# The second attention's scores in float32r: exact halves of q and k, copied through device memory

## The chip, the cores and the metric

One NeuronCore of a Trainium2 chip runs the whole program. The metric is the time of one execution on the device in microseconds. Engines are named as in the profile: PE (matrix products), PEld (its weight loads), DVE and ACT (element-wise work and reductions, both can read PSUM), POOL (GpSimd, SBUF only), SP (issues DMAs).

## The reference

An input `x` of 16 sequences of 256 tokens with 128 features goes through four residual layers: a first attention (2 heads of 64 features, rotated positions), a gated FFN, a second attention, and the same FFN once more.

```python
x = x + attn_a(layernorm(x))
x = x + ffn(layernorm(x))
x = x + attn_b(layernorm(x))
x = x + ffn(layernorm(x))
```

The second attention has 16 heads of 8 features. Its mask lets key k go with query q where k <= q, and a masked score is set to -10000. Cut to what matters:

```python
qkv = encodings @ attn_w.T + attn_b             # 16 heads of q, k, v with 8 features each
mask = arange(n)[:, None] <= arange(n)[None, :]
scores = einsum('bhki,bhqi->bhkq', k, q) / sqrt(8)
scores = where(mask, scores, -10000.0)
probs = softmax(scores, axis=2)                 # axis 2 is k: over the keys of each query
combined = einsum('bhkq,bhkl->bhql', probs, v)
out = combined.reshape(b, n, 128) @ out_w.T + out_b
```

The FFN has a hidden width of 512, three layers of ternary weights before the last product, and runs twice with the same weights.

## The kernel before, in words

Tokens are worked on in eight iterations of 512 (`TOK`), which are two sequences each (`s` = 0, 1). The residual `x` stays in SBUF (`XR`).

**A plan sets the order.** Nothing is issued as it is written. The body records operations with a guessed duration each, for example `p("PE", 1.2, ...)`. `Plan.laid` then places them in time on five engines, one after the other: an operation can start when its inputs have ended (plus `HOP`, or the `lag` given with it), its engine is free and a slot of its pool is free. Among those that could start on an engine about equally early it takes the one with the lowest number of `order_of`, which reads the table `ORDER`. `WEIGH` says how far a change of mode (an activation table on ACT, an array shape on PE) counts in this choice, `SWITCH` and `LOAD` what it costs. `p.either` leaves the choice between engines to the plan. `emit` then issues everything in that order, so each engine has a fixed queue. Since `emit` issues nearly all instructions, they all carry one line in the profile (L287), and operations are told apart by their tiles.

**Names in the profile.** Buffer numbers are left out, so `w` is a large work slot (`w4`, `w6`, `w8`) or a one-bank PSUM tile. `s` is the only score tile: four banks of PSUM, one slot, used by both attentions. `h` are the FFN's hidden parts, `h_sb` its weights, `hl` the FFN's last hidden layer, `m` the row maxima, `q` (with `s`) the tile `q2`.

**The FFN** splits its inputs into a rounded float32r part and the float32r rest (`parts`), and multiplies both with the float32r weights, in products of 512 columns. A branch at the end of the setup chooses between this and a version for weights that float32r can't hold; the execution profiled took the first.

**The second attention** (`attention_b_inputs`, `attention_b_max`, `attention_b`) has three steps in an iteration.

1. Inputs. A layernorm, a transpose, and the products of q, k and v in f32, each evicted from a PSUM bank. Four heads share 32 rows (8 features each). To single out one head, k is evicted four times, each time scaled by a mask `kmask` that leaves one head's features, with extra rows set to one; q is evicted twice (`qscale`). These tiles sit in `g_16` (q) and `g_32` (k).
2. Maxima, per sequence. For each of four head positions `a`: scores of four groups `g` at once, in four bands of 32 rows of the array (f32, 128 queries by 128 keys and 128 by 256), then a bf16 product with `hide` that adds a very negative number where the mask forbids. DVE reduces the tile to negated maxima (`m3`). When all four are done, small operations bring the maxima into `nm`, PE transposes it, and DVE adds it into the free rows of q, which gives `q2`.
3. Probabilities and sums, per sequence. Scores again, transposed (keys on the partitions) from k and `q2`, so that the maximum is subtracted by the product itself; ACT takes the exponential of the tile, POOL's `affine_select` zeroes what is masked on the diagonal blocks, and PE sums with `vp`.

A tile of scores holds three blocks of 128 by 128 per head (the fourth is all masked). The tiles of steps 2 and 3 take turns on the one score tile; the plan puts products of the FFNs (first `f`, then `g`) on PE in the waits.

**DMA queues.** SP issues the loads at the start and one store of `x` per iteration at the end. POOL issues the loads of the weights that are rounded to float32r on the way. After the loads nothing but the stores moves through DMA.

Of the kernel before, what the change touches and what calls it, by code (L numbers as in the profile page):

```python
# [94 lines left out]
class Plan:  # L95
# [4 lines left out]
    SWITCH = 0.15  # L100
    WEIGH = 0.78
# [64 lines left out]
    def laid(self):  # L166
# [28 lines left out]
        for _ in range(len(self.ops)):  # L195
            best = None
            for e, ops in ready.items():
# [23 lines left out]
                if not cands:  # L221
                    continue

                first = min(a + self.WEIGH * c for a, c, _ in cands)
                at, cost, op = min(
                    (x for x in cands if x[0] + self.WEIGH * x[1] <= first + 0.144),
# [63 lines left out]
class _Recorder:  # L290
# [47 lines left out]
    (INPUT, "a"): (47, 0.9),  # L338
    (MAIN, "a"): (52, 1.0),
    (NORM, "f"): (298, 0),  # L340
    (FILL, "f"): (118, 3.3),
    (INPUT, "b"): (76, 0.9),
    (MAXIMA, "b"): (-22, 0),
    (MAIN, "b"): (14, 17.0),
    (NORM, "g"): (81, 0),
    (FILL, "g"): (180, 9.1),
}
LATER_AT = -89
# [23 lines left out]
def hybrid_kernel(ctx: ExitStack, tc: tile.TileContext, x, rows, cols, wa, wb, w12, h1, h2, w3, out):  # L372
# [5 lines left out]

    p = Plan(nc)
# [13 lines left out]
    g_24, g_16, g_32 = group("w6", 4), group("w4", 3), group("w8", 3)  # L393
    q_qkv, q_pT, q_qkT, q_qb, q_pa, q_kb = Group(2), Group(3), Group(2), Group(2), Group(2), Group(2)
    g_rope, g_oT, g_small = group("rope", 6), group("oT", 2), group("small", 16)
    g_vb, g_q2, g_wv, g_o, g_oTb = (group(n, k) for n, k in (("vb", 2), ("q2", 2), ("wv", 2), ("o", 2), ("oTb", 1)))
# [166 lines left out]

    pi = fixed([P, 4], "pi", I32)
    p("POOL", 0.1).iota(pi[:], pattern=[[0, 4]], base=0, channel_multiplier=1)
    wanta = fixed([P, 4], "wanta", I32)
    p("POOL", 0.1).iota(wanta[:], pattern=[[1, 4]], base=0, channel_multiplier=0)
    wantr = fixed([P, 4], "wantr", I32)
    p("POOL", 0.1).iota(wantr[:], pattern=[[-3, 4]], base=31, channel_multiplier=0)
    ai = fixed([P, 4], "ai", I32)  # L570
    ri = fixed([P, 4], "ri", I32)
    kmask = fixed([P, 4], "kmask")
    mrow4 = fixed([P, 4], "mrow4")
    kbias = fixed([P, 4], "kbias")
    qscale = fixed([P, 2], "qscale")
    qbias = fixed([P, 2], "qbias")
    mrow = fixed([P, 2], "mrow")
    s8 = 1.0 / math.sqrt(DB)
    o = p("DVE", 1.25)
    o.tensor_scalar(ai[:], pi[:], 3, 3, ALU.arith_shift_right, ALU.bitwise_and)  # L580
    o.tensor_scalar(ri[:], pi[:], 31, None, ALU.bitwise_and)
    o.tensor_tensor(kmask[:], ai[:], wanta[:], ALU.is_equal)
    o.tensor_tensor(mrow4[:], ri[:], wantr[:], ALU.is_equal)
    o.scalar_tensor_tensor(kbias[:], kmask[:], cols_sb[:, C_BK : C_BK + 1], mrow4[:], ALU.mult, ALU.add)
    o.tensor_scalar(qscale[:, 0:1], kmask[:, 3:4], -s8, s8, ALU.mult, ALU.add)
    o.tensor_scalar(qscale[:, 1:2], kmask[:, 3:4], s8, None, ALU.mult)
    o.tensor_scalar(qbias[:], qscale[:], cols_sb[:, C_BQ : C_BQ + 1], None, ALU.mult)
    o.tensor_reduce(mrow[:, 0:1], mrow4[:, 0:3], AX.X, ALU.max)
    o.tensor_copy(mrow[:, 1:2], mrow4[:, 3:4])
# [137 lines left out]
    def attention_a(i, qkv, qkT):  # L727

        sc = p.tile(psum, [P, SEQS, HA, 2, T], F32, f"sa{i}", g_scores)
        for s in range(SEQS):  # L730
            o = p("PE", 0.87, "2r")
            for q in range(2):
                for h in range(HA):
                    hs = slice(h * DA, (h + 1) * DA)
                    c0 = s * T + q * P
                    o.matmul(
                        sc[:, s, h, q, :],
                        lhsT=qkT[hs, 0, c0 : c0 + P],
                        rhs=qkT[hs, 1, s * T : (s + 1) * T],
                        start=True,  # L740
                        stop=True,
                    )
# [59 lines left out]
    def attention_b_inputs(i):  # L802

        xT = layernorm_T(i, "b", ob[:])
        q = sb([P, 2, TOK], f"qb{i}", g_16, q_qb)
        pq = bank(f"pqb{i}", ahead)
        p("PE", 0.45, "1", claim=[q]).matmul(pq[:], lhsT=wb_sb[:, 0:128], rhs=xT[:], start=True, stop=True)
        for c in range(2):
            by, plus = qscale[:, c : c + 1], qbias[:, c : c + 1]
            p.either(  # L810
                ("DVE", 0.72, "tensor_scalar", (q[:, c, :], pq[:], by, plus, ALU.mult, ALU.add), {}),
                ("ACT", 0.67, "activation", (q[:, c, :], pq[:], AF.Identity), {"bias": plus, "scale": by}),
            )
        k = sb([P, 4, TOK], f"kb{i}", g_32, q_kb)
        pk = bank(f"pkb{i}", ahead)
        p("PE", 0.45, "1", claim=[k]).matmul(pk[:], lhsT=wb_sb[:, 128:256], rhs=xT[:], start=True, stop=True)
        for a in range(4):
            by, plus = kmask[:, a : a + 1], kbias[:, a : a + 1]
            p.either(
                ("ACT", 0.67, "activation", (k[:, a, :], pk[:], AF.Identity), {"bias": plus, "scale": by}),  # L820
                ("DVE", 0.72, "tensor_scalar", (k[:, a, :], pk[:], by, plus, ALU.mult, ALU.add), {}),
            )
# [8 lines left out]
        return q, k, v  # L831

    def attention_b_max(i, s, q, k, v):
# [10 lines left out]
        for a in range(4):  # L844
            c = a // 3

            sc = p.tile(psum, [P, 4, 512], F32, f"sb{n}_{a}", g_scores)
            o = p("PE", 1.2, ("4r", "1"))
            for qt, c0, w in ((0, 0, P), (1, P, T)):
                for g in range(4):  # L850
                    gs = slice(32 * g, 32 * g + 32)
                    o.matmul(
                        sc[:, g, c0 : c0 + w],
                        lhsT=q[gs, c, t0 + qt * P : t0 + (qt + 1) * P],
                        rhs=k[gs, a, t0 : t0 + w],
                        start=qt == 0,
                        stop=False,
                        skip_group_check=True,
                    )

            blocks = sc[:, :, 0:384].rearrange("p g (b k) -> p g b k", k=P)
            for g in range(4):
                o.matmul(
                    blocks[:, g, slice(0, 3, 2), :], lhsT=eye[:], rhs=hide[:], start=False, stop=True, skip_group_check=True
                )
            p("DVE", 1.68).tensor_reduce(
                m3[:, :, :, 3 - a].rearrange("p b g -> p g b"), blocks, AX.X, ALU.max, negate=True
            )
        nm = NMR[s]
        cols32 = nm[:].rearrange("p t (g r) -> p t g r", r=32)[:, :, :, 22:32:3]  # L870

        e0 = small([P, 2, 4, 4], f"e0{n}")
        m0 = small([P, 2, 4, 4], f"m0{n}")
        o = p("DVE", 0.4)


        o.tensor_scalar(cols32[:, 0], m3[:, 0], least[:, 0:1], None, ALU.min)
        o.scalar_tensor_tensor(cols32[:, 1], m3[:, 1], least[:, 1:2], m3[:, 2], ALU.min, ALU.min)
        o.tensor_scalar(m0, cols32, -NEG, None, ALU.min)
        p("ACT", 0.35, "exp").activation(e0, m0, AF.Exp, bias=neg[:])  # L880
        pm = bank(f"pm{n}")
        q2 = sb([P, 2, T], f"q2{n}", g_q2)
        o = p("PE", 0.15, "1", claim=[q2])
        for t in range(2):
            o.transpose(pm[:, t * P : (t + 1) * P], nm[:, t, :], ident[:])
        for c in range(2):
            p("DVE", 0.39).scalar_tensor_tensor(
                q2[:, c, :], pm[:, 0:T], mrow[:, c : c + 1], q[:, c, t0 : t0 + T], ALU.mult, ALU.add
            )
        return k, v, vp, e0, q2  # L890

    def attention_b(i, s, k, v, vp, e0, q2):
# [25 lines left out]
        for half in range(2):  # L918
            pTs = []
            for a2 in range(2):  # L920
                a = 3 - (2 * half + a2)
                c = a // 3


                st = p.tile(psum, [P, 4, 512], F32, f"st{n}_{a}", g_scores)
                blocks = st[:, :, 0:384].rearrange("p g (b q) -> p g b q", q=P)
                pT = sb([P, 3, 4, P], f"pT{n}_{a}", g_24, q_pT)
                o = p("PE", 0.66, "4r", claim=[pT])
                for kt, bs, w in ((0, slice(0, 3, 2), T), (1, slice(1, 2), P)):
                    for g in range(4):  # L930
                        gs = slice(32 * g, 32 * g + 32)
                        o.matmul(
                            blocks[:, g, bs, :],
                            lhsT=k[gs, a, t0 + kt * P : t0 + (kt + 1) * P],
                            rhs=q2[gs, c, T - w : T],
                            start=True,
                            stop=True,
                        )
                p("ACT", 1.38, "exp").activation(pT[:].rearrange("p b g q -> p g b q"), blocks, AF.Exp)
# [11 lines left out]
            for a2 in range(2):  # L951
                o = p("PE", 0.66, "4c", claim=[ps])
                for kt in range(2):
                    for g in range(4):
# [3 lines left out]
                            rhs=pTs[a2][:, slice(0, 3, 2) if kt == 0 else slice(1, 2), g, :],  # L958
# [42 lines left out]
    def product(po, w_sb, wv, os, high, low, nc_, claim, chain="ffn", part_of=None):  # L1001
# [15 lines left out]
        def general():  # L1017
            wl = []
            for c in range(nc_):
                wf = work.tile([P, P], F32, name="wf", tag="wf")  # L1020
                nc.sync.dma_start(out=wf[:], in_=wv[:, c, os])
                wl.append(work.tile([P, P], F32R, name=f"wl{c}", tag=f"wl{c}"))
                nc.gpsimd.tensor_tensor(wl[c][:], wf[:], w_sb[:, c, os].now(), ALU.subtract)
# [162 lines left out]
```

## Time and profile before

| | |
|---|---|
| time, median of 3 runs | 823.2 us (822.59 to 823.42) |
| the profiled execution | 823.35 us, of which its span is 821.6 us |
| granted clock of PE, mean | 0.983 |
| busy PE / DVE / ACT / POOL | 762.0 / 538.2 / 538.0 / 222.9 us |
| largest groups of PE | 281.2 us FFN products `w<-h,h_sb`; 71.4 us maxima scores `s<-w,w`; 71.2 us probability scores `s<-q,w`; 39.1 us mask `s<-hide,eye` |
| per score tile | 1755 ns reduction on DVE, 1452 ns exponential on ACT |
| table loads on ACT | 125, 160.4 us |
| DMA traffic | HBM read 8.53 MB, written 2.10 MB |

The span runs from the first to the last instruction. A group's row in the profile gives the line, the engine, the operation, output and inputs, the shape, the count, then busy time and mean duration of one, then the idle time before it and what ended that. Matmuls overlap with their successors, so the mean duration of one is longer than what it costs PE; the distance from start to start is the better measure. The rows of stages and of the order of time are explained where they are shown.

### The profile page before, as it was taken

What the parts mean: (1) busy time and instruction counts of PE and PEld (TensorE: products, weight loads), DVE (VectorE), ACT (ScalarE), POOL (GpSimd) and SP (SyncE); (2) the same over time, 40 slices, a digit from 0 to 9 for tenths busy, and PEclk for the clock granted to TensorE, in tenths of its full rate; (3) what the DMA queues carried; (4) which work ended last, traced back from release to release, by engine and by line L of the source; (5) the groups of instructions that cost most, each with busy time, mean ns of one, the idle gap of its engine ahead of it and who ended that gap; (6) DMA issues with size and microseconds to landing.
All of it is one profiled execution on the core that took longest, in us unless ns stands there. A gap on an engine that the chain in (4) does not pass through costs nothing.

```text
span 821.6 us, 15080 instructions
## 1 busy us (share of the span) xinstructions
PE 762.0 (93%) x6212; PEld 536.1 (65%) x6212; DVE 538.2 (66%) x1129; ACT 538.0 (65%) x744; POOL 222.9 (27%) x322
## 2 busy tenths in 40 slices
PE   4688999999999999999999998999999999999997
PEld 2355666667577676667675765776776577676775
DVE  7897866877778486637847775763773576262551
ACT  3455887745946746974687475549468546989743
POOL 7654444110411403320233033113113301323200
PEclk9689999999999999999999999999999999999999
DMA  9400000000000000000000000000000000000000
GB/s 286 130 2 1 1 2 0 2 1 1 2 1 1 1 2 1 1 2 1 1 2 2 1 1 2 2 14 2 14 1 14 2 1 14 1 14 1 14 15 18
DMA packets 12191, 11.69 MB, mean 14 GB/s; under 512 B 720, under 2 KB 9424, under 8 KB 12112
## 3 DMA queue, kind: packets, MB, share of 16 engines
q1 hardware_dynamic: 10624, 7.61, 3.0%
q0 software_dynamic: 1200, 2.62, 0.9%
q8 instruction: 51, 0.84, 0.4%
q10 hardware_dynamic: 288, 0.39, 0.3%
q14 instruction: 28, 0.23, 0.1%
HBM read 8.53 MB, written 2.10 MB: 13 GB/s over the span
## 4 chain that ended last, share of the span: by engine, by line
PE 60%; DVE 20%; ACT 14%; issue 2%; POOL 1%; DMA 1%; SPq 0%; POOLq 0%; DVEq 0%; ACTq 0%
PE w L287 45%; PE s L287 15%; ACT w L287 6%; ACT L287 5%; DVE w L287 4%; DVE h L287 2%; DVE small L287 2%; DVE xhattn L287 2%; ACT u L287 2%; DVE u L287 2%; DVE m L287 1%; DMA x<-in_x 1%; ACT h L287 1%; DVE o L287 1%; DVE xlffn L287 1%
## 5 line engine op out<-in xcount | busy, mean ns | idle before, releaser
L287 PE MATMUL w<-h,h_sb 128*128 128x512 f32 x1024 | 281.2, 412 | 3.7 <-DVE h L287 1.3
L287 PEld LDWEIGHTS w<-h,h_sb 128*128 128x128 f32 x1024 | 181.3, 189 | 56.0 <-issue 8.7
L287 ACT ACT_TABLE_LOAD x125 | 160.4, 1283 | 4.1 <-PEq L1177 1.3
L287 POOL TENSOR_SCALAR_AFFINE_SELECT w<-w 128x1024 f32<-128x1024 f32 x64 | 71.6, 1119 | 289.2 <-ACT w L287 282.9
L287 DVE TENSOR_REDUCE m<-s 128x12 f32<-128x1536 f32 x64 | 112.3, 1755 | 50.3 <-PE s L287 49.9
L287 ACT ACTIVATE u<-w,cols_sb 128x512 f32<-128x512 f32 x128 | 87.1, 687 | 76.5 <-PE w L287 75.9
L287 ACT ACTIVATE w<-s 128x1536 f32<-128x1536 f32 x64 | 92.9, 1452 | 32.1 <-PE s L287 30.7
L287 DVE TENSOR_TENSOR h<-u,h 128x512 fp32r<-128x512 f32 x105 | 74.9, 713 | 42.5 <-ACT h L287 39.8
L287 ACT ACTIVATE hl<-w,cols_sb 128x512 f32<-128x512 f32 x64 | 42.1, 687 | 53.7 <-PE w L287 53.4
L287 DVE SCALAR_TENSOR_TENSOR u<-w,cols_sb,u 128x512 f32<-128x512 f32 x64 | 47.7, 746 | 32.9 <-ACT u L287 26.6
L287 PE MATMUL s<-w,w 32*128 32x128 f32 (+1 forms) x1024 | 60.0, 348 | 3.9 <-DVE m L287 2.1
L287 PE MATMUL w<-w_sb,hl 128*128 128x128 f32 x512 | 63.1, 277 | 0.1
L287 PE MATMUL s<-q,w 32*128 32x256 f32 (+1 forms) x1024 | 59.8, 347 | 3.4 <-ACT w L287 2.7
L287 PEld LDWEIGHTS s<-q,w 32*128 32x128 f32 x1024 | 46.2, 184 | 25.5 <-ACT w L287 13.3
L287 PEld LDWEIGHTS w<-w_sb,hl 128*128 128x128 f32 x512 | 60.0, 192 | 2.8 <-ACT hl L287 1.9
L287 PE MATMUL w<-w,vp 128*32 128x256 f32 (+1 forms) x1024 | 55.3, 335 | 4.3 <-POOL w L287 2.8
L287 PE MATMUL w<-xTffn,w_sb 128*128 128x512 f32 x128 | 56.9, 445 | 2.2 <-DVE u L287 1.6
L287 DVE TENSOR_TENSOR x<-w,x 128x512 f32<-128x512 f32 (+1 forms) x40 | 23.2, 579 | 46.5 <-PE w L287 46.0
L287 PE MATMUL w<-xlffn,w_sb 128*128 128x512 f32 x128 | 52.5, 410 | 0.0
L287 PEld LDWEIGHTS s<-w,w 32*128 32x128 f32 x1024 | 34.3, 185 | 24.6 <-DVE m L287 8.9
L287 POOL TENSOR_TENSOR h<-u,h 128x512 fp32r<-128x512 f32 x23 | 29.6, 1290 | 65.3 <-ACT h L287 55.2
L287 PEld LDWEIGHTS w<-w,vp 128*32 128x32 f32 x1024 | 27.1, 110 | 29.5 <-issue 8.7
(153 smaller groups left out, 1068.2 us busy)
## 6 DMA issues: line engine op xcount, KB each, us to landing
w<-in_h SPq DMA_DIRECT2D x2, 1024.0 KB, 14.7
h_sb<-in_h POOLq DMA_DIRECT2D x2, 1024.0 KB, 11.6
out<-x SPq DMA_DIRECT2D x8, 256.0 KB, 2.3
x<-in_x SPq DMA_DIRECT2D x7, 256.0 KB, 8.0
w<-in_w SPq DMA_DIRECT2D x1, 512.0 KB, 8.8
w_sb<-in_w POOLq DMA_DIRECT2D x1, 512.0 KB, 7.2
rows_sb<-in_rows ACTq DMA_DIRECT2D x1, 384.0 KB, 7.1
x<-in_x SPq DMA_DIRECT2D x2, 128.0 KB, 3.2
```

The lines of the kernel that those rows point to most:

```text
L287: getattr(getattr(self.nc, self.ENGINES[op.engine]), name)(*a, **k)
```

## The change

The scores of the second attention are computed from float32r operands.

- **Halves.** q (already scaled by 1/sqrt(8) in its weights) and k are each evicted once into a float32r tile (the rounded part), and the rest is written beside it as a second float32r part. Two parts of q times two parts of k make four products.
- **Copies through device memory.** SP writes both parts, each twice, to a DRAM tile `far` (four DMAs per iteration, two for q and two for k). POOL reads `far` back (two DMAs per iteration) with rows ordered so that one head's 8 features stand in 32 rows four times, once for each pairing of parts. The result `t4` is `[P, 4, TOK]`: group `g` in the free dimension, head `a` in the band of 32 rows.
- **Scores.** All score products have 256 columns and use 32 rows; a tile of maxima has two sets of four, a tile of probabilities has two sets of four and two more that add the maxima: `pick` (ones in the rows of one group) times the transposed maxima `mT`, which are kept in two parts also. `q2`, `kmask`, `kbias`, `qscale`, `qbias` and `mrow` go.
- **Blocks.** The three used blocks of a tile stand next to each other in another order, so the mask is one run of 256 columns.
- **Pools.** `w8` has four slots in place of three and holds q and k; the small pool goes from 16 to 14 slots, the scratch of POOL's DMAs from 8192 to 4096. The branch for unrounded weights uses less memory.
- **The plan.** `ORDER`, `LATER_AT`, `WEIGH` (now by engine), `SWITCH` and the margin of equal starts have other values, and some guessed durations.

```diff
-    SWITCH = 0.15
-    WEIGH = 0.78
+    SWITCH = 0.17
+    WEIGH = {"ACT": 1.94, "PE": 0.13}
...
-                first = min(a + self.WEIGH * c for a, c, _ in cands)
+                weigh = self.WEIGH.get(e, 0.0)
+                first = min(a + weigh * c for a, c, _ in cands)
                 at, cost, op = min(
-                    (x for x in cands if x[0] + self.WEIGH * x[1] <= first + 0.144),
+                    (x for x in cands if x[0] + weigh * x[1] <= first + 0.038),
...
 ORDER = {
-    (INPUT, "a"): (47, 0.9),
-    (MAIN, "a"): (52, 1.0),
-    (NORM, "f"): (298, 0),
-    (FILL, "f"): (118, 3.3),
-    (INPUT, "b"): (76, 0.9),
-    (MAXIMA, "b"): (-22, 0),
-    (MAIN, "b"): (14, 17.0),
-    (NORM, "g"): (81, 0),
-    (FILL, "g"): (180, 9.1),
+    (INPUT, "a"): (-246, 24.6),
+    (MAIN, "a"): (-179, 7.8),
+    (NORM, "f"): (-106, 135.5),
+    (FILL, "f"): (-25, 25.2),
+    (INPUT, "b"): (47, 34.3),
+    (MAXIMA, "b"): (-415, 50.6),
+    (MAIN, "b"): (83, 10.6),
+    (NORM, "g"): (1714, 5.8),
+    (FILL, "g"): (1005, 103.1),
 }
-LATER_AT = -89
+LATER_AT = 124
...
-    g_24, g_16, g_32 = group("w6", 4), group("w4", 3), group("w8", 3)
+    g_24, g_16, g_32 = group("w6", 4), group("w4", 3), group("w8", 4)
...
     def attention_b_inputs(i):
         xT = layernorm_T(i, "b", ob[:])
...
-        for c in range(2):
-            by, plus = qscale[:, c : c + 1], qbias[:, c : c + 1]
+        tiles = []
+        for name, c0, bias in (("q", 0, C_BQ), ("k", P, C_BK)):
+            plus = cols_sb[:, bias : bias + 1]
+            pp = bank(f"p{name}b{i}", ahead)
+            hl = sb([P, 2, TOK], f"{name}hl{i}", g_16, q_hl, F32R)
+            p("PE", 0.45, "1", claim=[hl]).matmul(pp[:], lhsT=wb_sb[:, c0 : c0 + P], rhs=xT[:], start=True, stop=True)
             p.either(
...
+                ("ACT", 0.67, "activation", (hl[:, 0, :], pp[:], AF.Identity), {"bias": plus}),
+                ("DVE", 0.72, "tensor_scalar", (hl[:, 0, :], pp[:], plus, None, ALU.add), {}),
+            )
+            p("DVE", 0.77).scalar_tensor_tensor(hl[:, 1, :], pp[:], plus, hl[:, 0, :], ALU.add, ALU.subtract)
+            shape = [P, 2, 2, TOK]
+            far = p.fixed(dram.tile(shape, F32, name=f"far_{name}{i}"), shape)
+            for part in range(2):
+                p("SP", 0.55, lag=2.4).dma_start(
+                    out=far[:, part] if name == "q" else far[:, :, part],
+                    in_=hl[:, part, :].bitcast(F32).unsqueeze(1).to_broadcast([P, 2, TOK]),
+                )
+            t4 = sb([P, 4, TOK], f"{name}4{i}", g_32, None, F32R)
+            p("POOL", 0.85, lag=6.0).dma_start(out=t4[:], in_=far.rearrange("(g r) x y k -> (r x y) g k", g=4))
+            tiles.append(t4)
...
-        for a in range(4):
+        for g in range(4):
             sc = p.tile(psum, [P, 4, 512], F32, f"sb{n}_{g}", g_scores)
-            o = p("PE", 1.2, ("4r", "1"))
-            for qt, c0, w in ((0, 0, P), (1, P, T)):
-                for g in range(4):
+            o = p("PE", 0.28 + 0.15 + 0.42, ("4r", "1"))
+            for qt, c0 in ((1, 0), (0, T)):
+                for a in range(4):
+                    rows = slice(32 * a, 32 * a + 32)
                     o.matmul(
-                        sc[:, g, c0 : c0 + w],
-                        lhsT=q[gs, c, t0 + qt * P : t0 + (qt + 1) * P],
-                        rhs=k[gs, a, t0 : t0 + w],
+                        sc[:, a, c0 : c0 + T],
+                        lhsT=q[rows, g, t0 + qt * P : t0 + (qt + 1) * P],
+                        rhs=k[rows, g, t0 : t0 + T],
...
+        o.tensor_copy(both[:, :, :, 0:8:2].bitcast(F32R), m32)
+        o.tensor_tensor(both[:, :, :, 1:8:2].bitcast(F32R), m32, both[:, :, :, 0:8:2], ALU.subtract)
...
-        for c in range(2):
-            p("DVE", 0.39).scalar_tensor_tensor(
-                q2[:, c, :], pm[:, 0:T], mrow[:, c : c + 1], q[:, c, t0 : t0 + T], ALU.mult, ALU.add
-            )
+        evict(mT[:], pm[:, 0:T], T)
...
-                o = p("PE", 0.66, "4r", claim=[pT])
-                for kt, bs, w in ((0, slice(0, 3, 2), T), (1, slice(1, 2), P)):
-                    for g in range(4):
+                o = p("PE", 0.54, "4r", claim=[pT])
+                for kt, c0 in ((1, 0), (0, T)):
+                    for add in range(2):
+                        for a in range(4):
+                            rows = slice(32 * a, 32 * a + 32)
                             o.matmul(
-                            blocks[:, g, bs, :],
-                            lhsT=k[gs, a, t0 + kt * P : t0 + (kt + 1) * P],
-                            rhs=q2[gs, c, T - w : T],
-                            start=True,
-                            stop=True,
+                                st[:, a, c0 : c0 + T],
+                                lhsT=pick[rows, g, :] if add else k[rows, g, t0 + kt * P : t0 + (kt + 1) * P],
+                                rhs=mT[rows, :] if add else q[rows, g, t0 : t0 + T],
+                                start=kt == 1 and not add,
+                                stop=add == 1,
+                                skip_group_check=True,
                             )
```

## The prediction

> **What bounds the kernel now.** I read the page first, then the busy time by stage, then the groups of PE by shape, then the order of time around single score tiles, then the DMA issues.
>
> ```profile
> span 821.6 us, 15080 instructions
> PE 762.0 (93%) x6212; PEld 536.1 (65%) x6212; DVE 538.2 (66%) x1129; ACT 538.0 (65%) x744; POOL 222.9 (27%) x322
> ...
> PE   4688999999999999999999998999999999999997
> ```
>
> PE is the fullest engine and, after a ramp of about four slices, it has nines nearly to the end. The table of stages, cut where the second attention begins (its first scores at 169 us) and near its end, says how full:
>
> ```profile
> 0.00:164.00 164.00, 135.72 (x745) 89.04 (x745) 130.54 (x377) 106.33 (x247) 83.39 (x165) 0.93 0.17 53
> 164.00:779.00 615.00, 590.78 (x5285) 417.98 (x5285) 392.32 (x726) 413.94 (x472) 137.87 (x156) 1.00 0.01 4
> ```
>
> The columns are window, length, busy PE, PEld, DVE, ACT, POOL, then clock, DMA share and GB/s. In the 615 us that hold the second attention, PE idles 24.2 us. The granted clock is 1.00, the DMA engines are almost unused (0.01), and DVE and ACT are busy for two thirds. So this stage is PE's stage. A microsecond taken off PE there is worth a microsecond, as long as the planned order finds other PE work to put in its place.
>
> The order of time around one tile of the maxima (`s<-w,w`) and two tiles of the probabilities (`s<-q,w`) gives what PE spends on each:
>
> ```profile
> 401.01 0.94 PE L287 MATMUL s<-w,w 32*128 32x128 f32 x16
> 401.88 0.61 PE L287 MATMUL s<-hide,eye 128*128 128x256 bf16 x4
> 402.25 2.57 PE L287 MATMUL w<-h,h_sb 128*128 128x512 f32 x10
> 404.75 0.94 PE L287 MATMUL s<-q,w 32*128 32x256 f32 x16
> 405.62 0.65 PE L287 MATMUL w<-ident,xhattn 128*128 128x128 f32 x4
> ...
> 409.40 0.74 PE L287 MATMUL w<-h,h_sb 128*128 128x512 f32 x2
> 410.07 0.86 PE L287 MATMUL w<-w,vp 128*32 128x256 f32 x16
> ...
> 413.17 3.53 PE L287 MATMUL w<-h,h_sb 128*128 128x512 f32 x14
> 416.63 0.94 PE L287 MATMUL s<-q,w 32*128 32x256 f32 x16
> ```
>
> The first column is the start; start to next start is what PE gives away, since ends overlap. A maxima tile costs 0.87 us of scores (401.01 to 401.88), a probability tile 0.87 us (404.75 to 405.62). Each has eight program matmuls but 16 records: an f32 matmul runs as two instructions. The FFN's matmuls (`w<-h,h_sb`, rounded float32r operands) stand once each: 1024 for 16 FFNs of 64. Their pitch is the difference of two stretches, 14 in 3.46 us and 2 in 0.67 us: 12 in 2.79, so 0.233 us for 512 columns.
>
> **The change part by part.** *Scores on PE.* Read one by one in the trace, the sets of four concurrent matmuls of the maxima tile start at 401.014, 401.227, 401.339 and 401.557, and the mask begins at 401.884. A 256-column set takes 0.218, a 128-column set 0.109; what remains is 0.104 at the start (first weights) and 0.109 at the end (change of array shape): 0.104 + 2x0.109 + 2x0.218 + 0.109 = 0.867. The probability tile is the same sum in another order.
>
> After the change every set is 256 columns of float32r, in one instruction. For such a set with 32 rows the trace has no row. It is bounded below by the bf16 mask's 0.109 for 256 columns and above by the f32 set's 0.218. I take 0.116, half of the FFN's 0.233, as that row has the same type. A maxima tile has two sets: 0.104 + 0.232 + 0.109 = 0.445, a saving of 0.42. A probability tile has four (two products, two additions of the maxima through `pick`): 0.104 + 0.464 + 0.109 = 0.677, a saving of 0.19. With 64 tiles each: 27.0 + 12.2 = 39.2 us off PE. The ends: 41 us (0.109), 0 (0.218). The mask, the transposes, the products of q, k, v and the weighted sums keep number and shape.
>
> *ACT and DVE.* Six evictions of q and k per iteration go (DVE 13.3 + 6.4, ACT 11.2 + 6.1 = 37.0 us in their rows); in come 16 ACT evictions at 0.687 (the row `hl<-w,cols_sb`) and 16 DVE subtractions at 0.746 (the row `u<-w,cols_sb,u`), 22.9 us. The two additions into `q2` (14.1 us) become one copy of 256 columns, 16 at about 0.4. Two more small operations per sequence at about 0.2 are 6.4 us. Net some 15 us less on engines that are two thirds busy: I count nothing. In the chain from maxima to probabilities the 0.4 of small operations replaces one 0.48 addition: nothing again.
>
> *The trip through device memory.* Per iteration SP issues four writes of 512 KB, POOL two reads of 1 MB: 32 MB in eight iterations. The nearest rows:
>
> ```profile
> h_sb<-in_h POOLq DMA_DIRECT2D x2, 1024.0 KB, 11.6
> out<-x SPq DMA_DIRECT2D x8, 256.0 KB, 2.3
> x<-in_x SPq DMA_DIRECT2D x7, 256.0 KB, 8.0
> ```
>
> The last figure is us from issue to landing. `out<-x` ran on quiet engines; the other two in the opening rush, when the first of 40 slices moved 286 GB/s. At that rate 256 KB more is 0.9 us, so a lone write is about 3.2 us and the second of a pair, behind it, some 1.8 later. The plan books 2.4. A quiet read is estimated as 2.3 + 768 KB at 286 GB/s = 5.0, the plan books 6.0. The loaded rows would give 8.0 and 11.6. I take the quiet ones, because the DMA share of this stage is 0.01 and the new traffic, 4 MB or 15 us in about 77 us per iteration (615/8), is spread.
>
> What a late landing does: the read waits in POOL's queue for its two writes. Behind it stand the `affine_select`s of the probabilities, and PE's weighted sums wait for those. The first scores of an iteration wait on PE for the read itself. In the trace q's product precedes the iteration's first maxima by 5, 10 and 16 us in the first three iterations and by 53 us or more in the other five. With four slots of `w8` and two per iteration the next q and k can still be fetched one iteration ahead, so in five of eight the trip is covered. About 1 to 2 us late in three iterations: 4 us, between 0 and the second rival's price. The issues (16 on POOL at 0.78, 32 on SP at 0.37) lie on queues with room; SP has only eight output stores behind them, none needed by an engine.
>
> Here two pages of the Trainium skill speak against the change. "DMA: Bandwidth & Descriptors", section "Anatomy of one DMA", puts a transfer at about 2.0 us plus bytes over 436 GB/s and warns that completion is slow above all for writes to HBM; it would give 2.6 us for the 256 KB store, which took 2.3 here, and 3.2 and 4.4 for the new transfers, which leaves the sum as it is. "SBUF — State Buffer", section "SBUF: two separate sides", says that DVE in a fast two-port mode keeps GpSimd from writing descriptors, 3.1 us in place of 0.62; no run here shows that yet, and at 2.5 us for each read the forecast would be up to 40 us worse if nothing covered it.
>
> *The order.* All planned places, weights of a change of mode and pool sizes change too. PE idles 24.2 us in the long stage and 28.3 us before it; a better order could win some of that, a worse one lose as much. I count 0 and put 16 us either way into the range. The setup operations (under 2 us) and the shortened branch for unrounded weights, which no instruction of this trace comes from, count nothing.
>
> **Sum.** The profiled execution took 823.35 us for a span of 821.6, 0.15 above the median of 823.2. 823.35 - 39.2 + 4 = 788.
>
> **The rivals.** *The order packs better still.* DVE and ACT are relieved, and a third of the 52.5 us of PE's idle time goes as well, some 17 us: 771. For: ACT spends 160.4 us on 125 table loads, and the weight of a table load in the plan more than doubles. Against: 96% is already high.
>
> *ACT becomes the bound in places.* In the stage 697 to 738 us ACT is busy 38.79 of 41.00, in 328 to 369 36.12. There PE's saving buys nothing unless the plan moves evictions to DVE. If half of the 39.2 is lost: 823.35 - 19.6 + 4 = 808. Against: DVE has 19.46 and 20.18 in those two windows.
>
> *The trip lands late (slower).* If the loaded rows hold, a write is 5.6 us late (8.0 against 2.4) and a read 5.6 (11.6 against 6.0). Eight stalls of POOL with selects and PE behind them are 45 us, three uncovered reads 17 more: 823.35 - 39.2 + 62 = 846. It decides from 39.2/8 = 4.9 us of standing PE per iteration. For: the queues are in order, with no way round a wait. Against: quiet engines, and the early inputs.
>
> *One pass is not one pass.* If a 32-row float32r set takes the f32 set's 0.218, a maxima tile saves 0.22 and a probability tile, with its four sets, loses 0.22: nothing, and 4 us of the trip, 827. Against it stands the FFN's pitch with the same type; for it, that this row has 128 rows.
>
> **How the numbers follow.** Forecast 0.58 (788, its own range 776 to 800), better order 0.13 (771), half lost to ACT 0.12 (808), late trip 0.12 (846), no single pass 0.05 (827). A measurement of this kernel can tell about 0.2%, 1.6 us, from no change. The first three cases are faster, 0.83; the last two slower; of these, 0.02 is for a late trip that just cancels the gain. So faster 0.83, same 0.02, slower 0.15. The range takes the first three cases with their spread, 766 to 814, and leaves out 0.17.
>
> **What would show it.** Right: PE busy near 723 us, 512 fewer PE instructions, sets of the score tiles 0.11 to 0.13 apart, landings near 3 to 5 us for writes and 5 to 6 for reads, and hardly a wait of PE for POOL or a DMA. Wrong: sets at 0.2 or more; POOL waiting several us for device memory with selects behind it; PE's idle time in the long stage above 30 us; ACT over 38 of 41 us in several windows.

## The result, and the profile after

The changed kernel is slower: 850.92 us (median of 4 runs, 850.31 to 852.41) against 822.89 beside it, a ratio of 1.035 (95% interval 1.032 to 1.038). The forecast was 788, its range 766 to 814. The profiled execution took 850.31 us for a span of 848.6.

The page of the changed kernel, in the rows shown of the kernel before:

```profile
span 848.6 us, 16238 instructions
PE 794.8 (94%) x6724; PEld 569.0 (67%) x6724; DVE 543.8 (64%) x1161; ACT 496.3 (58%) x681; POOL 250.2 (29%) x350
...
PE   4788988899989999999999999999999999999996
```

PE was to lose 512 instructions and some 39 us. It has gained 512 (6212 to 6724) and 32.8 us. DVE and ACT together do 36.1 us less, 16.7 of it table loads (160.4 to 143.7). The table of stages says that PE is even fuller than before in the long stage, at the same clock:

```profile
0.00:164.00 164.00, 132.61 (x738) 87.46 (x739) 131.79 (x381) 94.30 (x222) 82.08 (x163) 0.96 0.17 53
164.00:779.00 615.00, 601.41 (x5639) 433.92 (x5638) 385.10 (x731) 365.57 (x414) 162.55 (x182) 1.00 0.16 58
```

So PE does not wait more; it works more. The groups of PE's score products, by shape, show where:

```profile
L288 PE MATMUL w<-h,h_sb 128*128 128x512 f32 x1024 | 271.9, 407 | 5.6 <-ACT u L288 1.6 <-DVE h L288 1.6 <-DVE w L288 1.1
L288 PE MATMUL s<-w,w 32*128 32x256 f32 x2048 | 154.2, 400 | 5.9 <-ACT w L288 3.4 <-DVE m L288 2.5
...
L288 PE MATMUL s<-mT,pick 32*128 32x256 f32 x512 | 61.8, 463 | 0.0
```

The column to look at is the count. The program issues 512 products of q and k for the maxima and 512 for the probabilities; `s<-w,w` has 2048 records, two for each, as an f32 product has. The 512 products of `pick` and `mT` have 512 records, one each, as the FFN's float32r products. (The profile prints f32 as the shape's type for both; the count tells them apart.) In order of time, a maxima tile, then a probability tile:

```profile
280.68 1.15 PE L288 MATMUL s<-w,w 32*128 32x256 f32 x16
281.76 0.61 PE L288 MATMUL s<-hide,eye 128*128 128x256 bf16 x4
282.12 0.48 PE L288 MATMUL w<-xTffn,w_sb 128*128 128x512 f32 x1
...
314.40 0.71 PE L288 MATMUL s<-w,w 32*128 32x256 f32 x8
314.75 0.48 PE L288 MATMUL s<-mT,pick 32*128 32x256 f32 x4
315.05 0.61 PE L288 MATMUL s<-w,w 32*128 32x256 f32 x8
315.30 0.48 PE L288 MATMUL s<-mT,pick 32*128 32x256 f32 x4
315.71 0.66 PE L288 MATMUL w<-ident,xhattn 128*128 128x128 f32 x4
```

The maxima tile with its mask takes 1.44 us (280.68 to 282.12; before 1.24, the median over all 64 tiles in both), the probability tile 1.31 (314.40 to 315.71; before 0.865). That is 64 x (0.208 + 0.446) = 41.8 us more of PE. Read one by one, a set of q and k runs as two instructions 0.216 apart: 0.432 us for 256 columns, where 0.116 was predicted.

One row names the reason. It is the first half of q or k, as ACT or DVE writes it, and beside it the maxima:

```profile
491.37 0.75 DVE L288 TENSOR_SCALAR w<-w,cols_sb 128x512 f32<-128x512 f32 x1 [0.66 <-PE w L288]
...
494.98 0.37 ACT L288 CAST mT<-w 128x256 fp32r<-128x256 f32 x1
```

The maxima are written as fp32r; the "rounded" half of q is written as f32. The plan's slots decide that, in code that the diff leaves as it was:

```python
if slot not in group.homes:
    kind = F32R if dtype == F32R else F32
    group.homes[slot] = pool.tile([shape[0], group.words], kind, name=f"{group.tag}{slot}")
home = group.homes[slot][:, 0:words]
if dtype not in (F32, F32R):
    home = home.bitcast(dtype)
```

A slot is declared by its first user. The first users of `w4` and `w8` are the first attention and the weights of the setup, all f32. A later float32r tile in such a slot gets the f32 buffer, with no word said: PE multiplies q4 and k4 as f32, the first half is all of q and the second should hold nothing (no run shows its values). `mT`, `pick` and `h` have pools or buffers of their own and are float32r.

The trip through device memory, in the DMA issues:

```profile
far_q<-w SPq DMA_DIRECT2D x16, 512.0 KB, 4.8
far_k<-w SPq DMA_DIRECT2D x16, 512.0 KB, 5.0
w<-far_q POOLq DMA_DIRECT2D x8, 1024.0 KB, 6.7
w<-far_k POOLq DMA_DIRECT2D x8, 1024.0 KB, 8.7
```

The last figure is the median time from issue to landing in us. These medians are later than the estimates (3.2 for a lone write, 5.0 for a read); the quickest write took 2.7 and the quickest read 5.9. Yet in this kernel the only wait for any of them is 0.5 us, on POOL.

### The profile page after: what moved, and what is told of

Its sections match the earlier page's. It is cut to its first block, busy times and chain, and to the rows that moved or that the text cites. A ratio compares the mean times of both kernels' runs of the same rounds, so it can differ in the third digit from the quotient of the medians.

```text
span 848.6 us, 16238 instructions
## 1 busy us (share of the span) xinstructions
PE 794.8 (94%) x6724; PEld 569.0 (67%) x6724; DVE 543.8 (64%) x1161; ACT 496.3 (58%) x681; POOL 250.2 (29%) x350
## 4 chain that ended last, share of the span: by engine, by line
PE 74%; DVE 14%; ACT 6%; issue 3%; POOL 1%; DMA 1%; SPq 0%; DVEq 0%; ACTq 0%; POOLq 0%
PE w L288 52%; PE s L288 22%; DVE w L288 3%; ACT w L288 3%; DVE small L288 2%; ACT L288 2%; DVE u L288 1%; DVE h L288 1%; DVE m L288 1%; DVE xhattn L288 1%; DVE xhffn L288 1%; DMA x<-in_x 1%; ACT u L288 1%; DVE stattn L288 1%; POOL rope L288 1%
## 5 line engine op out<-in xcount | busy, mean ns | idle before, releaser
L288 PE MATMUL w<-h,h_sb 128*128 128x512 f32 x1024 | 271.9, 407 | 5.6 <-ACT u L288 1.6
L288 PE MATMUL s<-w,w 32*128 32x256 f32 x2048 | 154.2, 400 | 5.9 <-ACT w L288 3.4
L288 ACT ACT_TABLE_LOAD x112 | 143.7, 1283 | 16.9 <-DVE small L288 9.0
L288 PEld LDWEIGHTS s<-w,w 32*128 32x128 f32 x2048 | 86.9, 184 | 47.7 <-issue 17.3
L288 DVE TENSOR_TENSOR h<-u,h 128x512 fp32r<-128x512 f32 x94 | 66.8, 713 | 24.3 <-ACT h L288 21.8
L288 POOL TENSOR_TENSOR h<-u,h 128x512 fp32r<-128x512 f32 x34 | 43.5, 1290 | 119.0 <-ACT h L288 117.5
L288 PE MATMUL s<-mT,pick 32*128 32x256 f32 x512 | 61.8, 463 | 0.0
L288 PEld LDWEIGHTS w<-w,vp 128*32 128x32 f32 x1024 | 26.9, 109 | 29.0 <-issue 15.1
L288 PE MATMUL w<-ident,w 128*128 128x128 f32 x192 | 32.5, 301 | 13.8 <-DVE w L288 12.0
```

The costliest lines, as they stand in the source:

```text
L288: getattr(getattr(self.nc, self.ENGINES[op.engine]), name)(*a, **k)
```

## The experiments

Theory A: the slots' type makes the score products f32, and the extra PE time is the loss. Theory B: 32-row sets take two passes whatever their type. Theory C: the trip through device memory sets the time. All experiments that keep "the order untouched" give the plan the same durations and dependencies, so every engine has the same queue.

**e1, the control.** It leaves out the branch for unrounded weights, as e2 and its variants do.

> The changed kernel with only the branch for unrounded weights left out, which no execution here enters: the partner of the next run, with the same plan. All theories: 848 to 853 us, as the changed kernel; 16 records for the products of q and k in each score tile.

850.76 us: no difference. It serves as the partner of e2.

**e2, float32r tiles.**

```diff
...
-            if slot not in group.homes:
-                kind = F32R if dtype == F32R else F32
-                group.homes[slot] = pool.tile([shape[0], group.words], kind, name=f"{group.tag}{slot}")
-            home = group.homes[slot][:, 0:words]
-            if dtype not in (F32, F32R):
-                home = home.bitcast(dtype)
+            kind = F32R if dtype == F32R else F32
+            if group.tag == "w8":
+                home = pool.tile([shape[0], group.words], kind, name=f"w8{name}", tag=f"w8{slot}")[:, 0:words]
+            else:
...
+                if dtype != group.kinds[slot]:
+                    home = home.bitcast(dtype)
...
```

> The same plan and the same order as e1, but each user of a w8 slot gets a buffer declared with its own type, so that q4 and k4 are really float32r (in the changed kernel the slot keeps the type of its first user, float32), and the halves are written as float32r. Theory A (the changed kernel multiplies q4 and k4 as float32, in two instructions of 0.216 us a set, because of the slots' type): the product records halve, 2048 to 1024; a maxima tile falls from 1.44 to about 0.82 us of PE, a probability tile from 1.31 to about 0.70, some 78 us of PE in all, and the time to between 772 and 805. Theory B (32-row sets take two passes whatever their type): no change, 848 to 853. Theory C (the late trip through device memory sets the time): PE falls, but the time by less than a third of it, above 825.

803.68 us, 47.1 less than e1 and 2.2% faster than the kernel before (ratio 0.978, 0.974 to 0.982). Theory A holds, B falls, and so does C's forecast for this run, above 825. A tile of each kind in order of time:

```profile
460.77 0.51 PE L292 MATMUL s<-w8k,w8q 32*128 32x256 f32 x8
461.21 0.61 PE L292 MATMUL s<-hide,eye 128*128 128x256 bf16 x4
461.57 0.71 PE L292 MATMUL w<-h,h_sb 128*128 128x512 f32 x2
...
597.12 0.39 PE L292 MATMUL s<-w8q,w8k 32*128 32x256 f32 x4
597.35 0.29 PE L292 MATMUL s<-mT,pick 32*128 32x256 f32 x4
597.47 0.29 PE L292 MATMUL s<-w8q,w8k 32*128 32x256 f32 x4
597.58 0.28 PE L292 MATMUL s<-mT,pick 32*128 32x256 f32 x4
597.80 1.44 PE L292 MATMUL w<-h,h_sb 128*128 128x512 f32 x5
```

Eight records of q and k in a tile where there were sixteen; 0.807 us with the mask in place of 1.445, and 0.674 in place of 1.311 (medians): 81.6 us of PE. The sets of the probability tile stand 0.11 to 0.12 apart, where the prediction had 0.116. So f32 costs more than the records say: twice as many, and a set takes 0.432 in place of some 0.117, 3.7 times as long. But only 47.1 of the 81.6 us became time, 0.58 of it. The pages of e1 and e2 show where a part of the rest is:

```profile
span 849.1 us, 16208 instructions
PE 796.6 (94%) x6724; PEld 569.6 (67%) x6724; DVE 545.1 (64%) x1161; ACT 496.5 (58%) x681; POOL 251.1 (30%) x350
...
span 801.6 us, 14160 instructions
PE 730.1 (91%) x5700; PEld 515.3 (64%) x5700; DVE 550.4 (69%) x1161; ACT 495.8 (62%) x681; POOL 249.5 (31%) x350
```

PE's busy time falls by 66.5 us and not by 81.6, and its idle time (span less busy) rises from 52.5 to 71.5. The last section has one reason for the first, stretches at half clock.

**e3, no unread columns**, in the changed kernel (f32).

```diff
-            for qt, c0 in ((1, 0), (0, T)):
+            for qt, c0, w in ((1, 0, T), (0, T, P)):
...
-                        rhs=k[rows, g, t0 : t0 + T],
+                        rhs=k[rows, g, t0 : t0 + w],
...
-                for kt, c0 in ((1, 0), (0, T)):
+                for kt, c0, w in ((1, P, P), (0, T, T)):
```

> The changed kernel with its order untouched, but without the columns that nobody reads: the set of maxima for the first 128 queries has 128 keys in place of 256, the sets of probabilities for the last 128 keys 128 queries in place of 256. Theory A: 64 x (0.218 + 0.218 + 0.055) = 31 us off PE, which is nearly all that the tiles cost more than before; time 818 to 826. Theory C: less than half of that comes back, above 835.

830.16 us. The tiles fall to 1.234 and 1.096 us, 27.2 us of PE, and the time by 20.6 against e1: between the two expectations. So 27.2 of the 41.8 us of extra PE time were in the fourth block of each score tile, which the change computes to have 256 columns and which f32 pays in full.

**e4, without `pick`**, in the changed kernel.

```diff
...
-                    for add in range(2):
+                    for add in range(1):
...
```

> The changed kernel with its order untouched, but without the products of pick and the transposed maxima, so the probabilities are not shifted by their maxima (that part of the computation is left out). These sets are float32r in the changed kernel too, one record each. Theory A: 64 x 2 x 0.116 = 15 us off PE, time about 836 (833 to 840), which is also a measure of what a one-pass set costs. Theory B: a set costs 0.218, 28 us, about 823. Theory C: under 7 us.

840.98 us, 1 us outside theory A's 833 to 840. The probability tile falls by 0.235, two sets at 0.118: 15.0 us of PE, as theory A has it, and 9.8 us of time against e1. Again a fraction, 0.65. With e3's 27.2 this makes 42.2 us, all of the 41.8: on the blocks that are needed, the f32 products of q and k cost what they did before, and what came on top is the fourth block and `pick`.

**e5, e2 without the unread columns** (the edit of e3 on e2).

> e2 (float32r tiles, 803.7 us) with its order untouched and without the columns that nobody reads, as in e3: one set of a maxima tile and two sets of a probability tile (one of the products, one of pick) have 128 columns. If a float32r set of 128 columns costs half of one of 256 (0.058), 64 x 3 x 0.058 = 11 us leave PE; at the rate at which e2 turned PE time into time (47.1 of 81.6 us, 0.58) that is 6 us: 797.5. If a short set costs as much as a long one: 803 to 805. If it takes more passes than a long one: over 810.

799.13 us, but the runs spread from 794.09 to 801.38 and e2's from 800.89 to 807.41. So the time decides nothing. PE lost 4.5 us, not 11: the maxima tile 0.057 of the expected 0.058, the probability tile 0.014 of 0.116. There the four sets now start 0.163, 0.112 and 0.171 apart (e2: 0.224, 0.119, 0.117): what the first short set saves (0.061), the long set behind the short one of `pick` takes back (0.054). That the loads of the next weights are the reason was not shown.

**e6, e2 without `pick`** (the edit of e4 on e2).

> e2 with its order untouched and without the products of pick and the maxima, as in e4 (that part of the computation, the shift of the probabilities by their maxima, is left out). 64 x 2 x 0.112 = 14.3 us leave PE. If PE still bounds everywhere: 789.5. At the rate of e2 and e4 (0.58 to 0.65): 794 to 795.5. If the other engines bound by now: above 800.

799.58 us, between the second and the third expectation. PE lost 64 x 0.236 = 15.1 us and the time 4.1, a rate of 0.27. The four runs of e2 spread over 6.5 us and those of e6 over 4.5, so a rate of nearly 0 or of nearly 0.6 would fit as well. In the profiled executions PE's idle time rises from 71.5 to 80.2 us.

**e7, the kernel before without the mask products.**

```diff
...
-            for g in range(4):
-                o.matmul(
-                    blocks[:, g, slice(0, 3, 2), :], lhsT=eye[:], rhs=hide[:], start=False, stop=True, skip_group_check=True
-                )
+            p.use(o.op, eye[:], False)
+            p.use(o.op, hide[:], False)
```

> The kernel before with its order untouched, without the 256 mask products of its maxima tiles (the mask in the maxima is left out). 0.37 us of each maxima tile, 23.7 us in all, leave PE. If a microsecond off PE is a microsecond of time, as the prediction had it: 798.6. If part of it turns into waiting for DVE and ACT in an order that stays as it is, at 0.6: 808. If PE is not the bound: above 815.

805.07 us, 16.7 less than the kernel before beside it, for 23.7 us of PE: 0.70. So the prediction's step that a microsecond off PE is a microsecond of time was too high for the kernel before itself, in an order that stays as it is.

**e8, every read of q4 and k4 twice**, on e2.

```diff
...
-            p("POOL", 0.85, lag=6.0).dma_start(out=t4[:], in_=far.rearrange("(g r) x y k -> (r x y) g k", g=4))
+            o = p("POOL", 0.85, lag=6.0)
+            for again in range(2):
+                o.dma_start(out=t4[:], in_=far.rearrange("(g r) x y k -> (r x y) g k", g=4))
```

> e2 with its order untouched, but POOL reads each of the 16 tiles of q4 and k4 twice. The second read writes the same tile, so POOL stands until the first has landed (6 to 9 us) and the tile is ready that much later. Theory A (the trip is covered, e2 loses some 4 us by it): under 815. Theory C (the trip sets the time): 16 x 7 us of POOL standing with the selects behind it, above 850. In between: the cover of the first iterations is gone, three times 7 us, some 825.

915.99 us, 112.3 more than e2, which is 16 times 7.0: what theory C expected. The waits of that run (who waited for whom, us in total, times, longest):

```profile
PE w L292 <- POOL w L292: 108.7, 12, 17.7
...
POOL w8k L292 <- DMA w8k<-far_k: 60.6, 8, 10.5
...
POOL w8q L292 <- DMA w8q<-far_q: 52.4, 8, 8.4
```

POOL stands 113.0 us for the first reads, 7.0 us for each, in all eight iterations. PE stands 108.7 us behind POOL, most of it 13 to 18 us in each of seven iterations, where it needs what POOL's selects have masked. So here the work behind the reads was due at once and nothing covered them. The span grows by 110.3 us against e2's, 100.0 of it idle time of PE and 10.3 busy time for the same 5700 instructions.

A late write need not cost anything, though. In e11, the fastest kernel below, POOL stands once for 17.8 us (238 to 256 us) for a write:

```profile
POOL w8q L292 <- DMA far_q<-w: 17.8, 1, 17.8
```

Between 240 and 270 us PE has no wait over 0.15 us. Behind that read stood no select that PE needed yet. That e2 and the changed kernel lose little by the trip is thus because of where the reads are placed. In e2 all the waits for these transfers are these:

```profile
PE s L292 <- DMA w8k<-far_k: 2.0, 1, 2.0
...
POOL w8k L292 <- DMA far_k<-w: 1.8, 2, 1.3
...
POOL w8q L292 <- DMA far_q<-w: 0.2, 1, 0.2
```

**e9, e2 with the old places.**

```diff
-    SWITCH = 0.17
-    WEIGH = {"ACT": 1.94, "PE": 0.13}
+    SWITCH = 0.15
+    WEIGH = 0.78
...
-    (INPUT, "a"): (-246, 24.6),
+    (INPUT, "a"): (47, 0.9),
...
```

> e2 (float32r tiles, 803.7 us) with the planned places, the weights of a change of mode and the margin of the kernel before. If the new places are worth nothing, as the prediction counted them: 800 to 808. If they are worth up to the 16 us that it left open: up to 820. If the constants fit one program alone, so that a set taken from another one makes waits: above 820, with PE's idle time up by 20 us or more.

832.57 us, 28.9 more than e2 with the same work, and slower than the kernel before. Here the trip is exposed:

```profile
PE s L291 <- DMA w8k<-far_k: 10.4, 4, 3.8
...
POOL w8q L291 <- DMA far_q<-w: 7.1, 2, 5.5
...
POOL w8k L291 <- DMA far_k<-w: 1.2, 2, 0.8
```

That is 18.7 us of waiting beside 4.0 in e2. In the profiled executions PE idles 91.5 us in place of 71.5 and is busy 739.6 in place of 730.1 with the same 5700 instructions; it is also busy at half clock for 53.3 us in place of 35.0, which at twice the duration would be an estimated 9 of the 9.5. What made the other waits was not taken apart. On this evidence the constants belong to one program.

**e10, honest guesses**, in the changed kernel.

```diff
-            o = p("PE", 0.28 + 0.15 + 0.42, ("4r", "1"))
+            o = p("PE", 1.27, ("4r", "1"))
...
-                o = p("PE", 0.54, "4r", claim=[pT])
+                o = p("PE", 1.14, "4r", claim=[pT])
```

> The changed kernel (float32 products, 850.8 us), but with the guessed PE durations of its score tiles set to what they took: 1.27 and 1.14 us with a change of array shape of 0.17 on top, in place of 0.85 and 0.54. The plan then lays the same work out anew. If the too short guesses cost waits of their own: 835 to 845. If the order is PE's queue anyway and the work itself is the loss: 848 to 855. If the new order suits the other constants worse: above 855.

858.94 us, 8 more than the changed kernel. The short guesses are not what makes it slow; a new order from the same constants is a little worse.

**e11, e5 planned anew.**

```diff
-            o = p("PE", 0.28 + 0.15 + 0.42, ("4r", "1"))
+            o = p("PE", 0.22 + 0.15 + 0.42, ("4r", "1"))
...
-                o = p("PE", 0.54, "4r", claim=[pT])
+                o = p("PE", 0.43, "4r", claim=[pT])
...
-                p("SP", 0.55, lag=2.4).dma_start(
+                p("SP", 0.55, lag=3.4).dma_start(
...
-            p("POOL", 0.85, lag=6.0).dma_start(
+            p("POOL", 0.85, lag=7.6).dma_start(
...
-    (FILL, "g"): (1005, 103.1),
+    (FILL, "g"): (295.8, 186.6),
...
```

> e5 (float32r tiles, no unread columns, 799.1 us) with durations of the trip through device memory and of the score tiles as e2 showed them (writes 3.4, reads 7.6 after issue; PE 0.79 and 0.43), and places searched anew with them. If what keeps e5 from the 788 of the prediction is short waits of PE from an order made with other durations, and the half clock after them: 790 to 796, with fewer half-clock stretches than e5's eight after the start. If DVE and ACT bound by now: 797 to 803.

786.29 us (6 runs, 783.49 to 790.11), a ratio to the kernel before of 0.956 (0.953 to 0.958): faster than both kernels, and faster than either expectation had it. Which share of the 12.8 us against e5 is due to the durations and which to the places was not separated.

**e12, the kernel before planned anew**, with the same search.

> The kernel before with places searched anew, in the same way and for as long as for e11; the work is the same. If e11's gain over e5 comes from the search alone and would be had without float32r: 805 to 812. If the old places already suit the old work, and the search can win only what the lighter score tiles leave open: 818 to 827.

817.82 us, a ratio of 0.996 (0.995 to 0.997), 0.2 us below the range of "the old places already suit the old work". So this search alone wins some 3 us of e11's 36; the rest came only together with the changed work.

## Why the prediction was wrong, step by step

**The step that failed** is "After the change every set is 256 columns of float32r, in one instruction". It took the type from the diff (`F32R` in the call for `t4`) and did not follow it into the slot. The term was -39.2 us of PE; with f32 products it is +41.8. The f32 set was in the trace, the slot's rule in the unchanged code.

**The rival that named it was priced wrongly.** "One pass is not one pass" took 0.218 for a set and came to 827. But 0.218 is one of the two instructions of an f32 set, and so the upper end of the prediction's bounds for a float32r set was half of what an f32 set takes. With both, 0.432 a set, a maxima tile comes to 0.104 + 0.864 + 0.109 = 1.08 and a probability tile, with its two sets of `pick`, to 1.31, against 0.867: 64 x (0.21 + 0.44) = 42 us more, and at one to one 823.35 + 42 + 4 = 869. Its chance of 0.05 was for a property of the chip; that the products would not have the type that the diff asks for was not weighed.

**Had the type held**, the term would have been right: e2's tiles save 64 x (0.430 + 0.191) = 39.7 us against the kernel before, for 39.2 predicted. The set of 0.116 was measured as 0.11 to 0.12. (The upper end, given as 41 us, is 42 by the prediction's own sets.) e2's 803.7 is still 15.7 above the forecast of 788, and that is the next step.

**One to one was wrong.** Time follows PE's work by 0.70 (e7, from the kernel before), 0.65 and 0.76 (e4, e3, from the changed kernel), 0.58 (e2) and 0.27 (e6, from e2, with the spread named there). That all are below 1 is clear; that the rate falls as PE has less to do is not shown, as e6 alone would say so. The changed kernel's own 41.8 us became 28.0, which is 0.67, but there the order and the trip changed too. PE's idle time of 4% in the long stage looked like proof of a bound, yet taking work off PE left more idle time (e2, e6). Which engine it then waits for was not separated. In e2 PE's own half clock can be a part of the loss: from none between 200 us and the end in e1 it rises to 23.9 us, an estimated 10 to 12 us of PE beside the 34.5 that did not become time (last section). The prediction's rival of a half-lost gain, 808, is near where e2 came out (803.7), but not for its reason: ACT is busy over 38 of 41 us in none of e2's windows (at most 37.90, at 697 to 738 us).

**The order** was counted as 0 with 16 us either way. e9 says 28.9 for this work. In the changed kernel it was not tried by itself.

**The trip** was a right size by luck. 4 us were booked; e2 waits 4.0 in all, the changed kernel 0.5. But the medians of the landings came later than estimated, and the reason given does not hold. The leads of q's product over the first maxima (5, 10 and 16 us in the prediction; the trace before gives 3.9, 8.0 and 14.5) were those of the old order; in the changed kernel and in e2 the lead is 21 us or more in every iteration. And the cover claimed for five iterations of eight failed in e8: tiles ready 7 us later held up the selects in POOL's queue, and PE behind them, in seven of eight. The warning quoted from the Trainium skill, "SBUF — State Buffer", section "SBUF: two separate sides", of some 2.5 us more for a transfer that GpSimd issues, is not seen in the issues: they took 0.85 and 0.76 us of POOL, as the 0.78 of the loads before. Whether DVE was ever in the mode that the page speaks of, no run shows. The formula of "DMA: Bandwidth & Descriptors", section "Anatomy of one DMA", which stands there for transfers issued from GpSimd, gives an estimated 4.4 us for a read of 1 MB. Here the reads took 6.7 and 8.7 from issue to landing (e2: 6.3 and 8.0), none under 5.8, so the measurement decides. The writes of 512 KB, issued by SP, took 4.8 and 5.0 (e2: 3.2 and 4.4).

**ACT and DVE** lost 19.4 us besides table loads, for some 15 predicted. What that did to the time no run separates.

## What to carry to other kernels

Where buffers are shared, follow a type to the instruction that uses it, and count records: two for each matmul instead of one says f32 before any duration does. An engine that is 96% busy turned only part of what was taken off it into time here, 0.58 to 0.76 in the clear cases; planned anew (e11), the same work took 12.8 us less. A DMA issued from an in-order queue is as dangerous as the work behind its wait is urgent: 17.8 us of waiting cost PE nothing in e11, and 16 times 7 us cost some 110 in e8.

## What was not expected of the hardware

PE's granted clock falls to half after some short waits. The clock rows of the changed kernel and of e2 (a digit is a slice of 1/40 of the span, 9 is 90% or more):

```profile
PEclk9799999999999999999999999999999999999999
```

```profile
PEclk9699999999998999999999999999999999999999
```

In the clock records of e2 there are six stretches at 0.5 after 200 us, five of 3.4 and one of 6.8 us, 23.9 in all; the changed kernel has none before its end, the kernel before one of 3.4, e11 four of 3.4. Each of the first five in e2 begins within 2 us after a wait of PE of 1.3 to 2.3 us (210, 240, 327, 425, 497 us; the one at 497 is the wait for `w8k` shown at e8). Such a wait is no rule, though: one of 1.7 us in e2 (519 us) and three of 1.4 to 1.6 in the kernel before (264, 283, 508 us) are not followed by any, and the sixth stretch (634 us) has only waits of about 1 us and less before it. In these stretches of e2 PE is busy 23.2 of the 23.9 us, and the FFN's products stand 0.427 us apart in place of 0.234. So the stretches make PE's work longer, by an estimated 10 to 12 us; how much of that becomes time was not tried. The Trainium skill, "TensorE: Matmul & The Clock Gate", section "HAM oscillation — how this bites in real kernels", puts the limit at idle gaps of about 3.4 us; the length of the stretches, 3.4 us or twice that, fits its window, but here shorter waits preceded them.

And a short set can fail to save time. In e5 the 128-column set of `pick`, four float32r products at once in the middle of a probability tile, is followed by the next set after 0.11 us, where half of a 256-column set would be 0.058.
